# Two attentions: the first row maxima of the next step in front of this step's value products, and the low parts of queries and keys between a step's halves

## The chip, the core and the metric

The kernel is one program on one core of a Trainium2 chip. The metric is the time of one execution on the device, in microseconds (us), the median of several runs. Engine names are those of the profile: PE is TensorE (matmuls), PEld its weight loads, DVE is VectorE, ACT is ScalarE, POOL is GpSimd, SP is SyncE, which here issues DMAs only.

## What is computed

Two pre-norm transformer layers on an input of 16 batches x 512 positions x 128 values (float32). Layer 0 is causal attention (16 heads of 8) and a mixture of 8 experts of which each position takes two; layer 1 is attention without a mask and without an output projection, then a gated feed-forward network (FFN) on values rounded to 4-bit blocks. The change touches the two attentions alone:

```python
x = x + attn0(layernorm(x))    # layer 0
...
x = x + attn1(layernorm(x))    # layer 1
# attn0: q, k, v = split(x @ w_attn.T + b_attn)
#        w = softmax(where(tril, q @ k.T * 8**-0.5, -1e9));  (w @ v) @ w_proj.T + b_proj
# attn1: w = softmax((x @ w_Q) @ (x @ w_K).T / sqrt(8));      w @ (x @ w_V)
```

## The kernel before, in words

**Stages.** In time, the main loop of layer 0's attention fills about 100 to 850 us of the span, the experts 850 to 1215, layer 1's attention 1230 to 2010, the FFN the rest. Both attentions are built by the same function, `attention(layer)` (from line 558), with `causal` true for layer 0.

**Groups and steps.** The main loop (line 1256) goes over 64 groups: 16 batches, each with G = 4 groups of four heads. A group has NC = 4 steps `kc`, one for each chunk of 128 keys; the running number of a step is `now = NC * n + kc`. So a batch is 16 steps. A batch has two halves of two groups, each with its own tiles of queries and keys.

**Row maxima.** The softmax subtracts each row's exact maximum, which is found ahead: while the scores of group n are made, the maxima of group n + LEAD (LEAD = 3) are. `row_max` (from line 895) makes, for one chunk of 128 queries, matmuls `ps_max<-k,q` on 64 rows, two strips at a time, and DVE's `tensor_reduce` (L911) takes the maxima from PSUM to `mx`. In layer 0 two bf16 matmuls `ps_max<-mask_bf,ident_bf` add the mask to the last 128 columns. A chunk's maxima come in one or two *parts* (function `parts`), according to how many columns are left under the mask: one part holds both head pairs, if they fit into 512 columns together. In layer 1 there are always two. A step kc takes the chunk 3 - kc, so in layer 0 the maxima of steps 0 and 1 have two parts, of steps 2 and 3 one.

**From maxima to queries.** When a half's maxima are complete, `max_done` puts two things on the lists below: `part_max` (on DVE: `ml`, a copy and a difference that split the maxima into a high and a low part) and `put_max` (PE transposes `ps_mx`, an ACT copy and DMAs into spare rows of the query tile, so that the score matmul itself subtracts the maximum).

**Scores and values.** `score(kc, pairs)` makes two PSUM tiles `ps_sc` (64-row matmuls), then ACT's exponential `pt` (an `ACTIVATE`), and in layer 0 POOL's `affine_select` (L969), which zeroes what lies above the diagonal. `attend(kc)` is the value product: eight matmuls `ps_av<-pt,va` of 128 rows x 32 columns, in a tile `ps_av` that is held for a whole group; `leave` copies it to `av_sb` by ACT. `divide` (PE transposes to `ps_d`, DVE reciprocal and product) makes `at`. In layer 0 `turn_back` and `finish` make the output projection (`ps_t`, `ps_o`) and add it on DVE. In layer 1 `finish` is one POOL addition (L1041), followed two steps later by the LayerNorm and the quantization for the FFN (`quantize_after`; POOL's `ln_rstd` L204, `xn` L221, and `grid` L878).

**PSUM.** `for_dve` takes tiles of two banks from a ring of two (`ps_s`): all `ps_max`, `ps_d`, and in layer 0 also `ps_qk`, `ps_v`, `ps_o`, `ps_n`. `for_act` takes single banks from a ring of four (`ps_c`): `ps_sc`, `ps_av`, `ps_mx`, `ps_t`, in layer 1 also `ps_qk` and `ps_v`. A tile waits until the tile two (or four) places before it in its ring has been read.

**Who orders the work.** The helper `in_order` chains each instruction to the one before it on the same engine, so PE runs exactly in the order in which the Python code issues the matmuls, and POOL's larger operations likewise. In layer 0 DVE, ACT and POOL are chained wholly (`strict`); in layer 1 a scheduler places most of DVE's and ACT's instructions, while the reductions stay chained. Every matmul is recorded on line 294 (helper `mm`), every chained DVE or ACT operation on line 177, so that tiles, not lines, tell them apart.

**Lists of side work.** Everything that is not maxima, scores or value products hangs on three dictionaries by step: `soon` runs at the start of a step, `later` between the two halves of a step, `last_of` at its end. In layer 0 the prologue of batch b (LayerNorm `stats`, `moments`, `apply`; `both`, which makes `ps_qk` and the high parts `hi`; `low`, which makes the low parts `lo` on DVE from the same PSUM tile and sends them by DMA; and others) is entered at offsets from T = 16 (b - 2); `both` at T + 10 in `last_of`, `low` at T + 11 in `soon`.

**One step before the change**, in PE's order: `soon`; first part of the maxima of this step; first part of its scores; at kc = 2 the division of an earlier group (in layer 0 here, in layer 1 at the end of the step, by `last_of`); `later`; second parts of the maxima and scores; `last_of`; and then the value product of the step before (`behind`). The next step begins with its `soon` and its first maxima.

Of the kernel before, what the change touches and what calls it, by code (L numbers as in the profile page):

```python
# [36 lines left out]
def transformer_kernel(  # L37
# [25 lines left out]
    NC = S // P  # L63
# [79 lines left out]
    first = cp.tile([P, NE], F32, name="first")  # L143
# [165 lines left out]
    def table(name, shape, dtype=F32):  # L309
        return cp.tile(shape, dtype, name=name)  # L310

    steps = table("steps", [P, 1, NT], I32)
# [245 lines left out]
    def attention(layer):  # L558
        causal = layer == 0
# [28 lines left out]
        def for_dve(name):  # L588
            return ps_s.tile([P, 2, S], F32, tag="s", name=name)

        def for_act(name):
            return ring["act"](name)
# [294 lines left out]
        def strip(j):  # L887
            return slice(64 * j, 64 * (j + 1))
# [52 lines left out]
        def main_parts(b, g):  # L941


            hv = halves[b, g // 2]
            va = state[b]["va"]
            pts = {}
            acc = {}

            def score(kc, pairs):
                q0 = kc * P if causal else 0  # L950
                n = S - q0
                m = len(pairs)
                tiles = [for_act("ps_sc") for j in range(2)]
                for u, i in enumerate(pairs):
                    p = 2 * (g % 2) + i
                    for j, ps in enumerate(tiles):
                        r = strip(j)
                        mm(
                            ps[:, u * n : (u + 1) * n],
                            hv["k"][r, p, kc * P : (kc + 1) * P], hv["q"][r, p, q0:S],  # L960
                        )
                for j, ps in enumerate(tiles):
                    pt = pool.tile([P, S], F32, tag="pt", name="pt", bufs=12 if causal else 8)
                    act.activation(pt[:, 0 : m * n], ps[:, 0 : m * n], AF.Exp, scale=SCALE)
                    if causal:

                        head = pt[:, 0 : m * n].rearrange("p (u n) -> p u n", u=m)[:, :, 0:P]
                        in_order(
                            nc.gpsimd.affine_select(  # L969
                                head, head, pattern=[[0, m], [1, P]], base=0,  # L970
                                channel_multiplier=-1, compare_op=ALU.is_ge, fill=0.0,
                            ),
                            queue="pool",
                        )
                    for u, i in enumerate(pairs):
                        pts[kc, i, j] = pt[:, u * n : (u + 1) * n]

            def attend(kc):
                if kc == 0:
                    acc[0] = for_act("ps_av")  # L980
                av = acc[0]
                q0 = kc * P if causal else 0
                for i in range(2):
                    for j in range(2):
                        s = 2 * j + i
                        mm(
                            av[32 * s : 32 * (s + 1), q0:S],
                            va[:, kc, NP * j + 2 * g + i, :],
                            pts.pop((kc, i, j)),
                            start=kc == 0, stop=kc == NC - 1,  # L990
                        )

            def leave():
                t = pool.tile([P, S], F32, tag="av_sb", name="av_sb")
                act.copy(t, acc.pop(0))
                return t

            return score, attend, leave
# [25 lines left out]
        def finish(b):  # L1024
            at = state[b]["at"]
            xf = xs[b].rearrange("p c e -> p (c e)")
            if causal:
                aT = state[b]["aT"]
                ps = for_dve("ps_o")
                for c in range(NC):  # L1030
                    mm(ps[:, c // 2, EG * (c % 2) : EG * (c % 2 + 1)],
                       aT[:, c * P : (c + 1) * P], wo)
                p4 = ps[:, :, 0 : 2 * EG].rearrange("p b (c e) -> p b c e", e=EG)
                x4 = xs[b].rearrange("p (b c) e -> p b c e", b=2)
                vec.tensor_tensor(x4, x4, p4[:, :, :, 0:E], ALU.add)
                raw = state[b]["raw"]
                raws[b] = raw
                r4 = raw.rearrange("p (b c) e -> p b c e", b=2)
                vec.tensor_tensor(r4, r4, p4[:, :, :, E:EG], ALU.add)
            else:  # L1040
                in_order(nc.gpsimd.tensor_tensor(  # L1041
                    xf, xf, at.rearrange("p c e -> p (c e)"), ALU.add
                ), queue="pool")
            del state[b]


        LEAD = 3
# [7 lines left out]
        def max_steps(n):  # L1055
            if n >= len(groups):
                return []
            b, g = groups[n]
            return [
                [(lambda c=c, u=u: row_max(b, g, c, u)) for u in parts(c + 1)]  # L1060
                for c in reversed(range(NC))
            ]

        def max_done(n, step=None):
            if n < len(groups) and n % 2 == 1:
                at = groups[n][0], (n % G) // 2
                if step is None:
                    part_max(*at)
                    put_max(*at)
                else:  # L1070
                    soon.setdefault(step, []).append(lambda: part_max(*at))
                    later.setdefault(step + (not causal), []).append(lambda: put_max(*at))


        soon, later, last_of = {}, {}, {}
        pro = {}
        if causal:
# [43 lines left out]
            for b in range(2, B):  # L1121
                if b not in pro:
                    pro[b] = prologue(b)
                T = NC * G * (b - 2)
                for name, at, when in (
                    ("stats", -13, later), ("moments", -9, later), ("apply", 2, later),
                    ("biased", 3, later), ("turn", 6, later), ("values", 7, later),
                    ("both", 10, last_of), ("low", 11, soon), ("first", 13, later),
                    ("second", 16, later),
                ):  # L1130
                    if T + at >= 0:
                        when.setdefault(T + at, []).append(pro[b][name])
        else:
# [40 lines left out]
            rows = [f for n in range(LEAD) for fs in max_steps(n) for f in fs]  # L1174
# [72 lines left out]
        def quantize_after(b, step):  # L1247

            f = fp4_steps(b)
            for name, d in (  # L1250
# [2 lines left out]
            ):  # L1253
                later.setdefault(step + d, []).append(f[name])

        for n, (b, g) in enumerate(groups):
            nxt = n + LEAD
            steps = max_steps(nxt)
            score, attend, leave = main_parts(b, g)
            for kc in range(NC):  # L1260
                now = NC * n + kc
                maxima = steps.pop(0) if steps else []
                scores = [lambda u=u: score(kc, u) for u in parts(NC - kc)]
                for f in soon.pop(now, []):
                    f()
                if maxima:
                    maxima.pop(0)()
                scores.pop(0)()
                if kc == 2 and left:
                    bb, gg, t = left.pop(0)  # L1270
                    if not causal:
                        last_of.setdefault(now, []).append(lambda a=(bb, gg, t): divide(*a))
                    else:
                        divide(bb, gg, t)
                    if gg == G - 1 and causal:
                        later.setdefault(now + 1, []).append(lambda bb=bb: turn_back(bb))
                        at = now + 3
                        later.setdefault(at, []).append(lambda bb=bb: finish(bb))
                        gate_after(bb, at)
                    elif gg == G - 1:  # L1280
                        soon.setdefault(now + 1, []).append(lambda bb=bb: finish(bb))
                        quantize_after(bb, now + 1)
                for f in later.pop(now, []):
                    f()
                for f in maxima + scores:
                    f()
                for f in last_of.pop(now, []):
                    f()

                while behind:  # L1290
                    behind.pop(0)()
                behind.append(lambda kc=kc, f=attend: f(kc))
            behind.append(lambda b=b, g=g, f=leave: left.append((b, g, f())))
            max_done(nxt, NC * (n + 1))
        while behind:
            behind.pop(0)()
        for bb, gg, t in left:
# [499 lines left out]
```

## Time and profile before

| | before |
|---|---|
| median of 5 runs | 2254.33 us (2250.7 to 2255.74) |
| the profiled execution | 2254.83 us |
| its span in the profile | 2253.1 us |
| its granted TensorE clock | 0.964 |
| busy PE / PEld / DVE / ACT / POOL | 90 / 45 / 73 / 58 / 46% |
| the chain of work that ended last: PE / DVE / ACT / POOL | 36 / 13 / 4 / 2% |

The costliest groups of the attentions, with the page's columns: line, engine, operation, tiles, count, then busy us and mean ns of one, then idle time ahead of them and its commonest releaser:

```profile
L911 DVE TENSOR_REDUCE mx<-ps_max 128x2 f32<-128x1024 f32 (+1 forms) x896 | 1005.5, 1144 | 259.3 <-PE ps_max L294 256.7
L177 ACT ACTIVATE pt<-ps_sc 128x512 f32<-128x512 f32 (+2 forms) x1792 | 895.9, 570 | 442.4 <-PE ps_sc L294 413.0
L294 PE MATMUL ps_av<-pt,va 128*32 128x512 f32 (+3 forms) x4096 | 482.6, 530 | 11.7 <-POOL pt L969 8.1
```

A tile name on the left of the arrow is written, the names on the right are read; "128*32" is the shape of the weights on the array. The count is over the whole program, both layers. Matmuls are pipelined, so a duration on PE reaches into the next matmul; what a matmul costs the queue is read better from the interval between the starts of two that follow each other.

### The profile page before, as it was taken

How to read it: one execution, taken by the hardware profiler on the slowest of the kernel's cores; microseconds unless marked ns; L12 is line 12 of the kernel's file. 1: busy time of each engine (PE TensorE's matmuls, PEld its weight loads, DVE VectorE, ACT ScalarE, POOL GpSimd, SP SyncE). 2: the span in 40 equal slices, each digit the busy share in tenths (PEclk: the TensorE clock that was granted, in tenths of full speed). 3: DMA queues.
4: the chain of work that ended last, by engine and by line, in shares of the span. 5: the costliest groups of instructions: out<-in, count | busy, mean ns of one | idle time of the engine just before them, and what ended most of it. 6: DMA issues, size and time to landing. Idle time of an engine off the chain costs nothing.

```text
span 2253.1 us, 38218 instructions
## 1 busy us (share of the span) xinstructions
PE 2025.5 (90%) x13140; PEld 1019.3 (45%) x13140; DVE 1648.0 (73%) x2994; ACT 1299.0 (58%) x2564; POOL 1026.4 (46%) x1641
## 2 busy tenths in 40 slices
PE   6999999999999964989998999999999999995887
PEld 3444444444444432656665433333333333333665
DVE  6667676767767757946434888888888888845887
ACT  1566556656555642322334777777777777782443
POOL 3444746566574663132202355555455454115554
PEclk7999999999999976999999999999999999997999
DMA  7411222322222203555553222322222222100000
GB/s 191 113 60 60 77 78 88 94 75 73 66 76 83 58 25 99 148 154 143 157 152 98 69 69 78 92 82 72 85 69 68 69 69 70 57 2 3 22 24 28
DMA packets 148736, 180.15 MB, mean 80 GB/s; under 512 B 25647, under 2 KB 112784, under 8 KB 140352
## 3 DMA queue, kind: packets, MB, share of 16 engines
q1 hardware_dynamic: 139614, 160.26, 24.2%
q0 software_dynamic: 8352, 17.20, 2.7%
q8 instruction: 105, 1.72, 0.3%
q14 instruction: 87, 0.71, 0.1%
q10 hardware_dynamic: 578, 0.26, 0.1%
HBM read 116.55 MB, written 58.99 MB: 78 GB/s over the span
## 4 chain that ended last, share of the span: by engine, by line
PE 36%; DVE 13%; ACT 4%; POOL 2%; issue 1%; DMA 0%; SPq 0%; ACTq 0%; POOLq 0%
PE ps_av L294 10%; PE ps_sc L294 6%; PE ps_max L294 6%; DVE mx L911 5%; PE ps_y L294 4%; PE ps_h L294 4%; DVE hid L177 4%; ACT pt L177 3%; PE ps_d L297 2%; PE ps_qk L294 1%; POOL hid L177 1%; DVE f_mx L177 1%; PE ps_t L297 1%; DVE ml L177 1%; PE ps_v L294 1%
## 5 line engine op out<-in xcount | busy, mean ns | idle before, releaser
L911 DVE TENSOR_REDUCE mx<-ps_max 128x2 f32<-128x1024 f32 (+1 forms) x896 | 1005.5, 1144 | 259.3 <-PE ps_max L294 256.7
L177 ACT ACTIVATE pt<-ps_sc 128x512 f32<-128x512 f32 (+2 forms) x1792 | 895.9, 570 | 442.4 <-PE ps_sc L294 413.0
L294 PE MATMUL ps_sc<-q,k 64*128 64x512 f32 (+3 forms) x2048 | 479.3, 403 | 34.0 <-ACT pt L177 32.4
L294 PE MATMUL ps_av<-pt,va 128*32 128x512 f32 (+3 forms) x4096 | 482.6, 530 | 11.7 <-POOL pt L969 8.1
L294 PE MATMUL ps_max<-k,q 64*128 64x512 f32 (+3 forms) x2048 | 426.8, 433 | 26.2 <-DVE mx L911 19.1
L294 PEld LDWEIGHTS ps_max<-k,q 64*128 64x128 f32 x2048 | 185.8, 188 | 442.6 <-issue 175.4
L969 POOL TENSOR_SCALAR_AFFINE_SELECT pt<-pt 128x128 f32<-128x128 f32 (+1 forms) x768 | 247.2, 334 | 290.8 <-ACT pt L177 275.0
L294 PEld LDWEIGHTS ps_sc<-q,k 64*128 64x128 f32 x2048 | 230.1, 186 | 183.8 <-ACT pt L177 120.4
L1490 ACT ACTIVATE h<-ps_h,b1t 128x512 f32<-128x512 f32 x156 | 106.9, 687 | 192.7 <-PE ps_h L294 192.3
L1414 POOL DMA_INDIRECT got<-y_rows,backs x128 | 124.8, 975 | 99.5 <-DMA y_rows<-yt 63.6
L204 POOL TENSOR_TENSOR ln_rstd<-ln_ve,mhalf 128x4 f32<-128x4 f32 x62 | 63.9, 1030 | 202.6 <-DVE ln_nm L177 178.8
L294 PE MATMUL ps_y<-w2t,h 128*128 128x128 f32 x1248 | 148.6, 278 | 7.5 <-DVE yt L1504 7.5
L294 PE MATMUL ps_h<-xT,w1t 128*128 128x512 f32 x312 | 151.5, 618 | 2.5 <-DVE xT L305 1.3
L294 PEld LDWEIGHTS ps_y<-w2t,h 128*128 128x128 f32 x1248 | 144.4, 194 | 10.2 <-DVE yt L1504 8.0
L294 PEld LDWEIGHTS ps_av<-pt,va 128*32 128x32 f32 x4096 | 86.5, 108 | 137.3 <-issue 79.2
L533 POOL DMA_INDIRECT x_rows<-xg,slots x128 | 126.7, 990 | 25.5 <-issue 21.3
L294 PE MATMUL ps_max<-mask_bf,ident_bf 128*128 128x128 bf16 (+1 forms) x768 | 126.8, 248 | 0.0
L177 DVE SCALAR_TENSOR_TENSOR hid<-f_a,hid 128x704 f32<-128x704 f32 x64 | 78.6, 1229 | 22.5 <-ACT f_a L177 22.5
L297 PE MATMUL ps_d<-cst,av_sb 128*128 128x128 f32 x512 | 84.5, 288 | 6.7 <-DVE mx L911 5.2
L294 PEld LDWEIGHTS ps_h<-xT,w1t 128*128 128x128 f32 x312 | 51.1, 192 | 77.1 <-ACT h L1490 53.3
L294 PE MATMUL ps_gu<-wgT,xqT 128*128 128x352 f32 x128 | 53.7, 502 | 33.0 <-DVE hid L177 33.0
L177 ACT COPY av_sb<-ps_av 128x512 f32<-128x512 f32 x128 | 76.2, 595 | 11.4 <-PE ps_av L294 2.5
(242 smaller groups left out, 2140.9 us busy)
## 6 DMA issues: line engine op xcount, KB each, us to landing
q<-d SPq DMA_DIRECT2D x256, 128.0 KB
k<-d SPq DMA_DIRECT2D x256, 128.0 KB
d<-hi SPq DMA_DIRECT2D x64, 256.0 KB
d<-lo SPq DMA_DIRECT2D x64, 256.0 KB
xt<-x_rows SPq DMA_DIRECT2D x39, 262.0 KB
w1t<-in_w_dram SPq DMA_DIRECT2D x39, 256.0 KB
w2t<-in_w_dram SPq DMA_DIRECT2D x39, 256.0 KB
y_rows<-yt SPq DMA_DIRECT2D x39, 256.0 KB
```

What stands on the lines that cost most here:

```text
L177: ins = f(*args, **kw)
L204: in_order(nc.gpsimd.tensor_tensor(rstd, ve, mhalf, ALU.pow), queue="pool")
L294: return in_order(nc.tensor.matmul(out, lhsT, rhs, start=start, stop=stop))
L297: return in_order(nc.tensor.transpose(out, src, ident))
L533: ins = in_order(nc.gpsimd.indirect_dma_start(out=x_rows[:, :], out_offset=bass.IndirectOffsetOnAxis(ap=slots[:, b0 + u, k, c : c + 1], axis=0
L911: nc.vector.tensor_reduce(hv["mx"][:, c, :, p0 : p0 + m], s4, AX.X, ALU.max),
L969: nc.gpsimd.affine_select(head, head, pattern=[[0, m], [1, P]], base=0, channel_multiplier=-1, compare_op=ALU.is_ge, fill=0.0,),
L1414: ins = in_order(nc.gpsimd.indirect_dma_start(out=got[:, c, :], out_offset=None, in_=y_rows[0 : min(NT, NE * (b + 1)) * TS, :], in_offset= ...
L1490: nc.scalar.activation(h[:, f, :], ps, AF.Gelu, bias=t["b1"][:, f : f + 1])
```

## The change

The loop gets a helper `first_maxima(now)`, which runs `soon` of the step `now` and issues the first part of its maxima. It is called once ahead of the loop, and then, for the step now + 1, at the end of step now: after its scores and `last_of`, in front of the value product of the step before. In layer 1 the steps that end with a division (kc = 2, by `last_of`) keep the old order: there it is called after the value product (`turned`). `max_done` is called at the start of a group and not at its end. In layer 0 `low` goes from `soon` to `later`, so behind the first part of that step's maxima and of its scores. In layer 1 `finish` goes from `soon` to `later` of the same step.

```diff
-                    ("both", 10, last_of), ("low", 11, soon), ("first", 13, later),
+                    ("both", 10, last_of), ("low", 11, later), ("first", 13, later),
...
+        maxima = []
+        def first_maxima(now):
+            for f in soon.pop(now, []):
+                f()
+            n, kc = divmod(now, NC)
+            if kc == 0:
+                rows[:] = max_steps(n + LEAD)
+            if rows:
+                maxima[:] = rows.pop(0)
+                maxima.pop(0)()
+        rows = []
+        first_maxima(0)
         for n, (b, g) in enumerate(groups):
             nxt = n + LEAD
-            steps = max_steps(nxt)
             score, attend, leave = main_parts(b, g)
+            max_done(nxt, NC * (n + 1))
             for kc in range(NC):
                 now = NC * n + kc
-                maxima = steps.pop(0) if steps else []
                 scores = [lambda u=u: score(kc, u) for u in parts(NC - kc)]
-                for f in soon.pop(now, []):
-                    f()
-                if maxima:
-                    maxima.pop(0)()
                 scores.pop(0)()
...
-                        soon.setdefault(now + 1, []).append(lambda bb=bb: finish(bb))
+                        later.setdefault(now + 1, []).append(lambda bb=bb: finish(bb))
                         quantize_after(bb, now + 1)
                 for f in later.pop(now, []):
                     f()
                 for f in maxima + scores:
                     f()
+                maxima.clear()
+                turned = now in last_of and not causal
                 for f in last_of.pop(now, []):
                     f()
+                if not turned:
+                    first_maxima(now + 1)
                 while behind:
                     behind.pop(0)()
+                if turned:
+                    first_maxima(now + 1)
                 behind.append(lambda kc=kc, f=attend: f(kc))
             behind.append(lambda b=b, g=g, f=leave: left.append((b, g, f())))
-            max_done(nxt, NC * (n + 1))
```

## The prediction

> **What bounds the kernel now.** I read the busy table by stretches first, then the waits, then the timeline of single steps. Stretch 100 to 850 us is the causal attention of layer 0, 1230 to 2010 us the attention of layer 1; columns are stretch, length, then busy PE, PEld, DVE, ACT, POOL, clock, DMA share, GB/s.
>
> ```profile
> 100.00:850.00 750.00, 696.17 (x5365) 335.57 (x5357) 515.85 (x1166) 439.98 (x970) 432.67 (x995) 0.97 0.23 72
> 1230.00:2010.00 780.00, 734.04 (x4535) 292.94 (x4531) 672.57 (x1010) 603.71 (x1154) 358.65 (x404) 1.00 0.23 70
> ```
>
> TensorE is busy 93 and 94%, so its own order sets the end; in layer 1 VectorE (86%) and ScalarE (77%) have little to spare, in layer 0 they have much (69 and 59%). The reader is to see that a matmul saved counts at once in layer 0, and that in layer 1 every wait put in front of TensorE counts too. The waits view (waiter, releaser: sum us, mean ns, longest us) shows on whom TensorE waits: ScalarE's exponentials for `ps_sc`, VectorE's reduction for `ps_max`.
>
> ```profile
> PEld ps_max L294 <- DVE mx L911: 117.1, 173, 1.8
> PE ps_sc L294 <- ACT pt L177: 32.4, 121, 4.5
> ```
>
> The timeline (start, duration) of one causal seam between two steps, and of the maxima behind it:
>
> ```profile
> 446.43 0.87 PE L294 MATMUL ps_sc<-q,k 64*128 64x512 f32 x2
> 447.23 0.43 PE L294 MATMUL ps_av<-pt,va 128*32 128x128 f32 x8
> 447.58 0.45 PE L294 MATMUL ps_max<-k,q 64*128 64x384 f32 x2
> 447.96 0.28 PE L294 MATMUL ps_max<-mask_bf,ident_bf 128*128 128x128 bf16 x2
> 448.18 0.44 PE L294 MATMUL ps_sc<-q,k 64*128 64x384 f32 x2
> ```
>
> **What moves.** Set against each other engine by engine, the two programs have the same instructions. ScalarE, the DMA queues, the MoE and the FFN keep their order. TensorE has only the first maxima of a step and the value product in front of them swapped: in layer 0 at 153 seams directly and at 88 with another operation between them; in layer 1 at 182 seams of 242, the 60 with a division staying. VectorE has the low parts behind the first reduction at 14 places; GpSimd has the residual add of layer 1 (L1041) behind `ln_rstd`/`grid` instead of ahead, 15 times. So I price seams.
>
> **Layer 0, a plain seam.** Undisturbed intervals from start to start: before, `ps_sc` to `ps_av` .424, to `ps_max` .355, to the mask .371, to `ps_sc` .215, sum 1.365. After: `ps_sc` to `ps_max` .335 (as inside a step), to the mask .265, mask to `ps_av` .215 (not shown; taken as mask to `ps_sc`), `ps_av` to `ps_sc` .355 (as to `ps_max`): 1.170. The .195 are two changes of tile shape fewer, each about .1: three 64-row products in a row instead of two pairs. The other two seam kinds come out likewise, 2.119 to 1.919 and 1.578 to 1.373. Bounds of a seam: 0, if the mask pays the change that the maxima save, to .30, if mask to `ps_av` costs nothing of it. Of 153 seams, 14 are low steps and 17 wait for GpSimd; 122 x .195 = **-23.8 us** (0 to -37). The 88 others exchange like for like: nothing.
>
> **Layer 0, waits that go.** At 17 seams the product before 128x512 waits for `affine_select`:
>
> ```profile
> 461.33 1.40 PE L294 MATMUL ps_av<-pt,va 128*32 128x512 f32 x8
> 462.66 0.50 PE L294 MATMUL ps_max<-k,q 64*128 64x256 f32 x4
> ```
>
> With the maxima ahead (.433 + .322 with mask) the wait holds that work: 10 long ones x .755 + 7 short ones (.34 to .44) x .36 = **-10.1**. Five or six maxima that follow the product now wait .58 on VectorE's `ml`; in front they are fed earlier: **-3**. No wait is late next there: the slot that they need came free in the step before.
>
> **Layer 0, waits that come.** Low parts: today the product stands between the scores and the maxima that need VectorE's low parts.
>
> ```profile
> 285.41 1.41 DVE L177 SCALAR_TENSOR_TENSOR lo<-ps_qk,bp,hi 128x512 fp32r<-128x512 f32 x2 [2.88 <-ACT hi L177]
> 285.85 0.64 PE L294 MATMUL ps_av<-pt,va 128*32 128x256 f32 x8
> 286.88 0.50 PE L294 MATMUL ps_max<-k,q 64*128 64x512 f32 x2 [0.39 <-DVE lo L177]
> ```
>
> The changed order has the next maxima, and with them the `ps_s` slot that a low part holds, ahead of the product; queued behind them are the product and the next scores. The .57 that the product covered (285.85 to the maxima's unstalled start) comes back, 14 x .57 = **+8.0** (0 to +18: the upper end adds the reduction of 128x512, mean .69, that VectorE now does ahead of the low parts). The `ps_n` seams wait for the division's slot, 7 x .2 = **+1.4**; seams whose maxima wait for a VectorE slot already (14 x .25 = **+3.5**) and seams that gain just ahead of a GpSimd- or VectorE-limited place (10 x .2 = **+2**) lose their cover. Layer 0: -23.8 - 10.1 - 3 + 8.0 + 1.4 + 3.5 + 2 = **-22 us** (-34 to -8).
>
> **Layer 1, a plain seam.** Without a mask both orders have one 64-row block a step, so no shape change is saved (1.92 both ways). The step is paced by VectorE (2 reductions x 1.22 of a 3.19 us step), ScalarE (2 x .57 and copies) and two PSUM slots. Where the second scores wait for an exponential, maxima inside that wait gain .06. What moves is cover:
>
> ```profile
> 1538.32 1.26 POOL L878 TENSOR_TENSOR grid<-q_a,xn 128x512 bf16<-128x512 f32 x1
> 1538.44 1.19 DVE L177 CAST ml<-mx 128x32 fp32r<-128x32 f32 x1
> ...
> 1539.62 1.06 PE L294 MATMUL ps_av<-pt,va 128*32 128x512 f32 x8
> 1539.66 0.21 DVE L177 TENSOR_TENSOR ml<-mx,ml 128x32 fp32r<-128x32 f32 x1
> 1539.80 2.34 DVE L911 TENSOR_REDUCE mx<-ps_max 128x2 f32<-128x1024 f32 x2
> ...
> 1541.07 0.50 PE L294 MATMUL ps_max<-k,q 64*128 64x512 f32 x2 [0.38 <-DVE mx L911]
> 1541.40 0.39 PE L294 MATMUL ps_sc<-q,k 64*128 64x512 f32 x2
> ```
>
> The maxima at 1541.07 wait until the reduction begun at 1539.80 has freed their slot (about 1541.0). Today the product at 1539.62 runs inside that wait. Swapped, it stands behind it: maxima 1541.07, product 1541.43, scores 1542.43 instead of 1541.40, so 1.03 us lost; queued behind are the scores, both exponentials and `av_sb`. I replayed one batch (1535 to 1586 us) by hand, each tile at the latest of its engine, its slot and its input. In it this place loses 1.03, three others .19, .33 and .09 (an `ml`, a `q_a` and small slot waits), and later waits of .70 and .47 take .45 back: 1.19 a batch; the 14 batches between the first and the last x 1.19 = **+16.7** (0, if all is taken back as the .45 was, to +25, if nothing is).
>
> The residual add now comes to GpSimd directly behind `grid`, at 1539.58; VectorE's second `ml` operation comes at 1539.66. Where the two met in layer 0, VectorE took 1.22 for what takes .21 here:
>
> ```profile
> 408.22 1.27 POOL L800 TENSOR_TENSOR x<-x,b_bc 128x512 f32<-128x512 f32 x1
> 408.32 1.22 DVE L177 TENSOR_TENSOR ml<-mx,ml 128x32 fp32r<-128x32 f32 x1
> ```
>
> At the same boundary today (`grid`, then `xn`), 5 of 13 such `ml` operations were slowed. The add comes .08 ahead, so I take a little more, .45, at the full price: 13 x .45 x 1.08 = **+6.3** (0 to 14). The Trainium skill ("SBUF — State Buffer", section "SBUF: two separate sides") speaks against the change here: VectorE with two SBUF inputs and GpSimd share a port pair as an exclusive lock, and whichever starts first blocks the other for the whole instruction. By that rule the add, .08 ahead, would hold `ml` in every batch, and the sum would be 14 and not 6.3. Layer 1: 16.7 + 6.3 = **+23 us** (+5 to +33).
>
> **Sum.** -22 + 23 = +1 on the profiled execution's 2254.83 us (span 2253.1), .5 above the median 2254.33: **2256 us**, the gain of layer 0 paid back in layer 1. Own range 2247 to 2264.
>
> **Rivals.**
> - Regained (faster): in layer 1 the waits of the next steps absorb the late product. For it: the .45 regained in the replay, and 117.1 us of weight loads waiting on `mx`, so the reduction stream, not the product, paces some steps. Against: that stream is itself behind the late maxima. Layer 1 costs +6, layer 0 gives -22: 2239 (2236 to 2247).
> - Blocked and thin (slower): the add blocks `ml` in all 13 batches, +14, and layer 0 saves only 12, because the GpSimd chain behind its products (17 wait for it today) and VectorE's slots give gains back. One mechanism decides the sign: `ml` behind the add, just ahead of the reductions that feed layer 1's maxima; it decides once over 9 of 13 are blocked. 2254.8 - 12 + 30.7 = 2273.5 (2264 to 2277). For it: 408.22. Against: 8 of 13 went through beside `xn`.
> - The shape change isn't saved (the change doesn't do what it says): mask to `ps_av` takes .41, not .215, as the first product after 64-row scores does. Then -23.8 falls away: 2256 + 23.8 = 2280. Against: mask to `ps_sc` at .215 follows the same tile.
>
> **Numbers.** About .2%, 4.5 us, is what a measurement tells from no change. Forecast .42 (of it .09 faster, .20 same, .13 slower); regained .29, faster; blocked and thin .23, slower; not saved .06, slower. Faster .38, same .20, slower .42. The range 2236 to 2277 leaves out "not saved" and the tails of the bounds, about 2 in 10.
>
> **What would show it.** In layer 0 mask to `ps_av` near .2 and two batches in about 96.5 us (99.2 now); maxima of low steps waiting for `lo` with the product behind them. In layer 1 a batch period of 52.5 us, against 50.86 now, and the product behind the maxima in the place of 1539.62; `ml` at 1.2 in half of the batches. Wrong if layer 1's period stays, or if mask to `ps_av` is .4; and if ScalarE's waits for `ps_sc` grow in layer 0, a bound that I left out is at work.

## The result and the profile after

The changed kernel takes **2260.4 us** (median; 2254.0 to 2269.5) against 2254.65 before: ratio 1.0031, 95% interval 1.0023 to 1.0039. It is slower by .3%, just clear of what a measurement tells from no change. The forecast was 2256, its own range 2247 to 2264. The single number hides what happened; the two loops show it. Columns are stretch (first to last value product of a layer), length, busy PE, PEld, DVE, ACT, POOL, clock, DMA share, GB/s. Before:

```profile
64.88:821.96 757.08, 725.46 (x5599) 348.05 (x5597) 524.80 (x1141) 458.33 (x1009) 426.56 (x1016) 0.99 0.23 72
1225.37:2025.38 800.01, 752.00 (x4634) 298.92 (x4635) 677.13 (x1019) 619.07 (x1184) 362.86 (x407) 1.00 0.23 70
```

After:

```profile
65.28:781.97 716.69, 694.59 (x5592) 343.31 (x5591) 520.73 (x1140) 454.96 (x1008) 423.72 (x1014) 0.99 0.25 76
1185.93:2030.66 844.73, 782.94 (x4631) 307.91 (x4633) 687.83 (x1019) 612.09 (x1183) 361.06 (x407) 0.98 0.22 66
```

Layer 0 is **40.4 us shorter** (forecast -22) and layer 1 **44.7 us longer** (forecast +23). Both signs were right, and both sizes were forecast at about half of what came; both measurements lie outside the bounds that the prediction gave them (-34 to -8, +5 to +33). That the time came near 2256 is luck: the two errors, 18 us too little gain and 22 us too little loss, cancel.

The profiled execution took 2258.97 us, its span is 2257.3. Its waits follow, in the columns of the prediction's waits view (waiter, releaser: sum us, number of waits, longest us; the prediction takes the middle column for a mean, but it is a count). The first line is of the kernel before, the others of the changed one:

```profile
PE ps_max L294 <- DVE mx L911: 19.1, 44, 0.9
...
PE ps_sc L294 <- ACT pt L177: 39.4, 151, 4.5
PEld ps_max L294 <- DVE mx L911: 79.9, 130, 2.5
PE ps_max L294 <- DVE mx L911: 37.3, 39, 2.2
```

TensorE's own waits for VectorE's reduction went from 19.1 to 37.3 us, fewer and longer (39 of them, .96 each). In layer 1 alone they went from 13.3 to 28.0, so this wait grew by 14.7 us where the layer lost 44.7. The weight loads' share fell, so the sum over the program would have said little. The place is found by step. With a step counted as `now` mod 16 within a batch, and its length from the first scores of one step to those of the next, means over ten batches in the middle of each loop (us):

| kernel | layer 1: step 4 | 5 | 6 | the other 13 | ml's second operation |
|---|---|---|---|---|---|
| before | 3.36 | 2.90 | 3.98 | 40.7 | .21 to .40 |
| after | 5.68 | 3.81 | 3.53 | 41.3 | 1.20 to 1.21 |

and in layer 0, where a batch went from 49.50 to 46.82: step 4 -.43, 8 and 9 together -.67, 10 -.47, 11 -.60, 12 -.19, 15 -.15, all others within .11.

**Layer 0's seam**, in the timeline of TensorE (start, duration), after the change:

```profile
417.73 0.56 PE L294 MATMUL ps_sc<-q,k 64*128 64x512 f32 x2
418.07 0.40 PE L294 MATMUL ps_max<-k,q 64*128 64x384 f32 x2
418.40 0.28 PE L294 MATMUL ps_max<-mask_bf,ident_bf 128*128 128x128 bf16 x2
418.62 0.42 PE L294 MATMUL ps_av<-pt,va 128*32 128x128 f32 x8
418.97 0.45 PE L294 MATMUL ps_sc<-q,k 64*128 64x384 f32 x2
```

The product starts .22 after the mask, as forecast, and not .41: the shape change is saved. The second of the two score matmuls starts .07 after the first; from it to the next scores the seam takes 1.18. The prediction had 1.365 for it before the change and 1.170 after.

**Layer 1's place**, the step 4 of a batch:

```profile
1570.91 1.27 POOL L878 TENSOR_TENSOR grid<-q_a,xn 128x512 bf16<-128x512 f32 x1
1571.03 1.19 DVE L177 CAST ml<-mx 128x32 fp32r<-128x32 f32 x1
...
1572.15 1.26 POOL L1041 TENSOR_TENSOR x<-x,at 128x512 f32<-128x512 f32 x1
1572.26 1.20 DVE L177 TENSOR_TENSOR ml<-mx,ml 128x32 fp32r<-128x32 f32 x1
1573.39 3.47 DVE L911 TENSOR_REDUCE mx<-ps_max 128x2 f32<-128x1024 f32 x3
...
1574.66 0.50 PE L294 MATMUL ps_max<-k,q 64*128 64x512 f32 x2 [2.19 <-DVE mx L911]
...
1575.09 1.06 PE L294 MATMUL ps_av<-pt,va 128*32 128x512 f32 x8
```

Read it downward: both GpSimd operations hold one operation of `ml` each until they end (1572.18, 1573.41); the first reduction starts 2.4 us after `ml` began; the maxima wait 2.19 for it; and the product, which waits for nothing here, stands behind them with nothing of its 1.06 in the wait.

**The clock behind the wait.** Step 5 is longer for another reason. Here are steps 4 and 5 of this batch, and below them those of the batch two later, in the columns of the stretches above (the clock is the third number from the end, as a share of full speed):

```profile
1570.79:1576.09 5.30, 2.92 (x21) 1.01 (x18) 5.23 (x6) 2.06 (x4) 4.35 (x7) 1.00 0.00 0
1576.09:1580.41 4.32, 4.32 (x24) 1.57 (x21) 3.49 (x7) 3.17 (x6) 0.00 (x0) 0.60 0.02 6
1679.75:1685.04 5.29, 2.91 (x21) 1.01 (x17) 5.22 (x6) 2.06 (x4) 4.35 (x7) 1.00 0.00 0
1685.04:1687.96 2.92, 2.92 (x24) 1.21 (x21) 2.92 (x7) 2.78 (x6) 0.00 (x0) 1.00 0.00 0
```

In both, TensorE is busy through the whole of step 5 with the same work. At a granted clock of 0.60 it takes 4.32, at 1.00 it takes 2.92, which is the 2.90 of before. In the trace the clock stands at 0.50 for 3.41 us (1576.27 to 1579.68). Such a fall comes in 12 of the 16 batches of layer 1, each time after the wait for `ml`; in layer 1 of the kernel before there is none. The mid-loop batches with a fall take 54.4 to 54.6 us, the one without 53.03: 1.4 us a fall, so some 17 of the 44.7 us. The falls begin at whole multiples of 3.413 us from each other (1521.65, 1576.27 and 1630.88 are 16 x 3.413 apart), whatever the batch does, which may be why a wait of the same length is followed by a fall in one batch and not in another. No run sets the clock by itself: that the wait brings the fall is read from their order and from the counts below, and is not tested apart.

### The profile page after: what moved, and what is told of

The parts are those of the page before. It is cut to its first block, busy times and chain, and to the rows that moved or that the text cites. A ratio compares the mean times of both kernels' runs of the same rounds, so it can differ in the third digit from the quotient of the medians.

```text
span 2257.3 us, 38218 instructions
## 1 busy us (share of the span) xinstructions
PE 2025.6 (90%) x13140; PEld 1024.0 (45%) x13140; DVE 1655.7 (73%) x2994; ACT 1289.9 (57%) x2564; POOL 1022.6 (45%) x1641
## 4 chain that ended last, share of the span: by engine, by line
PE 41%; DVE 11%; ACT 4%; POOL 2%; issue 1%; DMA 0%; ACTq 0%; POOLq 0%; DVEq 0%
PE ps_av L294 11%; PE ps_sc L294 9%; PE ps_max L294 6%; PE ps_h L294 4%; PE ps_y L294 4%; DVE hid L177 4%; ACT pt L177 3%; DVE mx L911 2%; PE ps_d L297 2%; PE ps_qk L294 1%; DVE ml L177 1%; POOL hid L177 1%; DVE f_mx L177 1%; PE ps_t L297 1%; PE ps_mx L297 1%; PE ps_v L294 1%
## 5 line engine op out<-in xcount | busy, mean ns | idle before, releaser
L911 DVE TENSOR_REDUCE mx<-ps_max 128x2 f32<-128x1024 f32 (+1 forms) x896 | 995.3, 1143 | 214.9 <-PE ps_max L294 210.4
L294 PE MATMUL ps_sc<-q,k 64*128 64x512 f32 (+3 forms) x2048 | 520.4, 428 | 40.9 <-ACT pt L177 39.4
L294 PE MATMUL ps_max<-k,q 64*128 64x512 f32 (+3 forms) x2048 | 436.4, 414 | 42.7 <-DVE mx L911 37.3
L294 PEld LDWEIGHTS ps_sc<-q,k 64*128 64x128 f32 x2048 | 236.8, 187 | 451.2 <-ACT pt L177 311.7
L294 PEld LDWEIGHTS ps_max<-k,q 64*128 64x128 f32 x2048 | 203.1, 190 | 204.1 <-DVE mx L911 79.9
L177 DVE RECIPROCAL rec<-ps_d 128x16 f32<-128x16 f32 x128 | 32.6, 255 | 105.3 <-PE ps_d L297 105.2
```

Source lines behind the costliest of these rows:

```text
L177: ins = f(*args, **kw)
L294: return in_order(nc.tensor.matmul(out, lhsT, rhs, start=start, stop=stop))
L911: nc.vector.tensor_reduce(hv["mx"][:, c, :, p0 : p0 + m], s4, AX.X, ALU.max),
```

## The experiments

Two theories for layer 1. **Lock**: the residual add behind `grid` holds `ml`, and that is the loss. **Cover**: whatever `ml` takes, the maxima in front of the product wait with nothing beside them. For layer 0 the question was where 18 us more than forecast came from. All runs are against the kernel before on the same chip, its medians 2253.9 to 2254.2, but for the last two.

**One layer at a time.** Layer 0 alone, layer 1 in its old order:

```diff
-                turned = now in last_of and not causal
+                turned = not causal
...
-                        later.setdefault(now + 1, []).append(lambda bb=bb: finish(bb))
+                        soon.setdefault(now + 1, []).append(lambda bb=bb: finish(bb))
```

> Layer 0 as in the change, layer 1 in its old order (first maxima behind the value product, residual add ahead of grid). If the two layers act by themselves, as the stages of the two traces say (layer 0 shorter by 40, layer 1 longer by 45): 2254.7 - 40 = 2214 us. If a part of layer 0's gain is only work put off into the experts or layer 1: above 2222 us.

Measured 2217.7 us, ratio .9836 (.9812 to .9860). Layer 1 alone (`turned = causal or now in last_of`, `low` in `soon`):

> Layer 1 as in the change, layer 0 in its old order with the low parts in soon. If the layers act by themselves: 2254.7 + 45 = 2300 us, ml's second operation 1.2 us in nearly every batch. If layer 1's loss comes from what layer 0 leaves behind (its earlier end, the experts' reads): nearer to 2255 us.

Measured 2296.2 us, ratio 1.0185 (1.0171 to 1.0199). -36.6 and +41.9 make +5.3, close to the change's own 5.8: the layers act by themselves, and nothing is put off from one into the other.

**The add alone, and the swap without it.** The change with `finish` in `soon`:

> The whole change, but layer 1's residual add stays ahead of grid on GpSimd. Theory lock alone (the add behind grid holds ml's second operation, and this is all of layer 1's loss): 2260.4 - 45 = 2215 us. Theory cover alone (the first maxima wait for the reduction in front of the product, whatever ml takes): 2260 us. Both: ml's second operation back at 0.2 us, the reductions 1.0 earlier in 14 batches, so 2260.4 - 14 = 2246 us, with step 4 of a batch at 4.7 us (3.36 before, 5.68 after).

Measured 2241.4 us, ratio .9943 (.9928 to .9958). The kernel before with `finish` in `later` and nothing else:

> The kernel before with nothing but layer 1's residual add put behind grid. Theory lock alone: ml's second operation 1.2 us in nearly every batch and the whole loss of layer 1, 2300 us. Both: the product in front of the maxima covers what it can, but reductions that are 1.0 late can't be covered further, 2254.7 + 14 = 2269 us. Theory cover alone: 2255 us.

Measured 2267.2 us, ratio 1.0061 (1.0046 to 1.0075). Each theory alone is out; both act. The clock falls in seven batches of the first kernel and in one of the second. In this kernel the product stands in front of the maxima, and of the wait that `ml` makes it takes its 1.06:

```profile
1592.96 1.06 PE L294 MATMUL ps_av<-pt,va 128*32 128x512 f32 x8
1593.00 1.24 DVE L177 TENSOR_TENSOR ml<-mx,ml 128x32 fp32r<-128x32 f32 x1
...
1595.43 0.50 PE L294 MATMUL ps_max<-k,q 64*128 64x512 f32 x2 [1.40 <-DVE mx L911]
```

**The old order at one seam.** In layer 1 the product first wherever the maxima follow a split:

```diff
-                turned = now in last_of and not causal
+                turned = not causal and (now in last_of or now % 8 == 3)
```

> The whole change, but in layer 1 the two steps of a batch that follow a split of maxima (steps 4 and 12) keep the product in front of the maxima, as the steps with a division do. Theory lock and cover at step 4: step 4 falls from 5.68 to 4.3 and step 5 from 3.8 to 3.0, step 6 rises from 3.5 to 3.9, so 1.8 a batch: 2260.4 - 25 = 2235 us. Theory that every swapped step of layer 1 pays (cover lost all over): some 2 of 12 swapped steps, 2260.4 - 7 = 2253 us.

Measured 2259.2 us, ratio 1.0024 (1.0013 to 1.0036), step 4 still 5.68. A miss: this turns the seam that leads into step 4, and the wait falls at the seam out of it, as the prediction's own lines had it. With `now % 16 == 4` in its place:

> The whole change, but in layer 1 the one seam of a batch at which the wait falls (from step 4 to step 5) keeps the product in front of the maxima; in ml_turned the old order stood one step too early, and nothing moved. Theory cover at this seam: steps 4, 5 and 6 as in finish_alone (4.31, 3.03, 3.92; now 5.68, 3.81, 3.53), 1.76 a batch: 2260.4 - 25 = 2236 us. Theory that the lock alone makes step 4 late: 2258 us or more.

Measured 2240.9 us, ratio .9927 (.9907 to .9947): step 4 4.24, as expected, step 5 3.60 and not 3.03, step 6 3.53 and not 3.92. The clock falls in four batches (step 5 takes 4.06 to 4.21 there). In the others step 5 takes 3.35, and steps 4 to 6 together 11.11, against 11.17 in the kernel with the add alone and 11.74 in the changed one: the old order at this seam gives back what the swap had cost there, and step 5 only holds what step 6 held. One seam of a batch carries some 20 of the 45 us. By the batches with and without a fall, some 13 of these 20 are the clock (4 falls of .9 us in place of 12 of 1.4).

**No lock at all.** Layer 0 alone as above, and `grid` behind the four `xn` on GpSimd:

```diff
-                ("inverse", 10), ("scaled", 12), ("size", 14), ("least", 15), ("down", 15), ("grid", 16),
+                ("inverse", 10), ("scaled", 12), ("size", 14), ("least", 15), ("down", 15), ("grid", 18),
```

> The change in layer 0 alone, and layer 1 in its old order but with grid behind the four xn on GpSimd. If what is left of the lock (ml's copy, 1.19 beside grid) holds up step 4, it goes: step 4 from 3.38 to 2.9, 2217.7 - 7 = 2211 us. If the copy is hidden anyway: 2217 us.

Measured **2204.6 us**, ratio .9775 (.9762 to .9788), better than both kernels. `ml` takes .20 and .25, step 4 2.84, as step 12 does; step 6 falls to 3.54 too, which had not been expected. So the lock was in the kernel before already, for 11 us (its layer 1 goes from 800.0 to 788.8). The whole change with the same two GpSimd orders:

> The whole change in both layers, but on GpSimd the residual add stays ahead of grid, and grid comes behind the four xn, so that neither operation of ml meets a long GpSimd one. Theory that the cover is needed only because ml is held: the swap is nearly free in layer 1, step 4 near 2.9, and the small terms of the other steps (.6 a batch, 8 us) stay: 2204.6 + 9 = 2214 us. Theory that the cover is lost whatever ml takes: step 4 at 4.3 or more and 2204.6 + 28 = 2233 us.

Measured 2216.7 us, ratio .9834 (.9822 to .9847). With `ml` free the swap costs .50 at step 4 (3.34 against 2.84), and the clock doesn't fall:

```profile
1549.60 0.20 DVE L177 CAST ml<-mx 128x32 fp32r<-128x32 f32 x1
1549.84 0.25 DVE L177 TENSOR_TENSOR ml<-mx,ml 128x32 fp32r<-128x32 f32 x1
...
1551.27 0.49 PE L294 MATMUL ps_max<-k,q 64*128 64x512 f32 x2 [0.24 <-DVE mx L911]
```

Together the runs make a table of layer 1, first to last value product, with the number of falls of the clock in brackets. The last column is an estimate: it takes off each fall at what the batches with it took more than those without it in the same run (1.42 us in the swapped order, .9 in the old one).

| `ml` held by | old order | swapped | the swap costs | without the falls |
|---|---|---|---|---|
| nothing | 788.8 (0) | 803.6 (0) | 14.9 | 14.9 |
| `grid` | 800.0 (0) | 827.2 (7) | 27.2 | 17.3 |
| `grid` and the add | 813.8 (1) | 844.7 (12) | 31.0 | 14.8 |

Down a column the lock costs 25 in the old order and 41 in the swapped one; without the falls it is 24 in both, and the price of the swap hardly changes with the lock. That it seems to double is the clock. The falls go with the length of the wait ahead of step 4's last maxima: none where it is .6 us or less, four falls in 12 waits of 1.2 us (the old order at step 4's seam), one in 12 of 1.4 us (the add alone), seven in 12 of 1.4 us (the change with the add ahead of `grid`), and in the changed kernel eleven in 12 of 2.2 us and one more behind a wait of 1.4 us. Why equal waits of 1.4 us bring one fall in one run and seven in the other is open. Of the 14.9, .50 a batch are at step 4, and most of the rest at .07 to .18 in steps 2, 3, 10, 11, 14 and 15.

**The low parts.** The kernel before with `low` in `later`:

> The kernel before with nothing but the low parts put into later (the order of the maxima and products stays). Theory slot of the low parts (the prediction's: the next first maxima take the PSUM slot that the low parts read, wherever these stand): the low parts come .69 later behind a reduction and the maxima with them, 2254.5 + 14 x .7 = 2264 us. Theory slot by release (the maxima take the slot that is given back first in program order, which is now that of the 128-wide maxima): the .46 wait goes, 2254.5 - 6 = 2248 us, step 11 at 1.59 us as step 15 has it (2.04 before).

Measured 2254.4 us, ratio .9995 (.9986 to 1.0004): neither. The wait goes as the theory by release says (step 11 1.59), but step 12 gives it back (3.54, before 3.10): `ml` now stands behind the low parts on VectorE, and the transposes `ps_mx` wait for it. The change with `low` in `soon`:

> The whole change, but the low parts stay in soon, so ahead of the reduction of the 128-wide maxima. Theory slot by release: the next first maxima, now in front of the product, need the slot of the low parts, and wait for the second of them; step 11 goes from 1.44 to about 1.8 us or more, 2260.4 + 5 = 2265 us or more. Theory slot of the low parts (that wait is in the changed kernel already): not slower than 2260 us, rather 2251.

Measured 2279.7 us, ratio 1.0115 (1.0100 to 1.0131); step 11 2.61, far more than the 1.8 expected. Its lines:

```profile
419.98 1.41 DVE L177 SCALAR_TENSOR_TENSOR lo<-ps_qk,bp,hi 128x512 fp32r<-128x512 f32 x2 [1.65 <-ACT hi L177]
...
421.44 0.50 PE L294 MATMUL ps_max<-k,q 64*128 64x512 f32 x2 [0.95 <-DVE lo L177]
...
422.08 0.64 PE L294 MATMUL ps_av<-pt,va 128*32 128x256 f32 x8
```

And the changed kernel's:

```profile
413.94 0.69 DVE L911 TENSOR_REDUCE mx<-ps_max 128x4 f32<-128x512 f32 x1 [1.04 <-PE ps_max L294]
...
414.55 1.41 DVE L177 SCALAR_TENSOR_TENSOR lo<-ps_qk,bp,hi 128x512 fp32r<-128x512 f32 x2
...
414.89 0.45 PE L294 MATMUL ps_max<-k,q 64*128 64x512 f32 x2
```

Here the maxima start at 414.89, while the low parts read `ps_qk` until 415.96. They can't be in that slot: they have the one that the reduction gave back at 414.63. With the low parts ahead of the reduction in the code, the maxima get `ps_qk`'s slot and wait, with the product behind them. So the move of the low parts is worth nothing to the old order and 19 us to the new one.

**The projection behind step 10.** The change with the product first at layer 0's seam from step 9 to 10 (`turned = now in last_of and not causal or causal and now % 16 == 9`):

> The whole change, but in layer 0 the seam from step 9 to step 10 of a batch, after which queries and keys are projected, keeps the product in front of the maxima. Theory slot of ps_qk (its PSUM slot is given back by the reduction of these maxima, so maxima that come a product earlier free it earlier): ps_qk waits again, .95 us after ps_d instead of .49, and the seam's change of shape comes back, steps 9 to 10 up by .46 + .15 in 14 batches, 2260.4 + 8.5 = 2269 us. Theory that the projection's wait has another cause (ScalarE, the division): + .15 x 14 = 2262.5 us, with ps_qk at .49 after ps_d.

Measured 2374.3 us against 2347.5 of the kernel before on this chip, ratio 1.0118 (1.0098 to 1.0137). Once more:

> The kernel of qk_turned once more, since on the chip of that run the kernel before took 2347.5 us itself and layer 1 had a halt of some 7 us a batch that no other run shows. If layer 0's steps there (9 and 10 up by 1.22 a batch, ps_qk at .95) stand for themselves: 2260.4 + 14 x 1.22 = 2277 us here. If that chip's halt was also in them: 2269 us, as expected at first.

Measured 2363.0 against 2344.0 on another such chip, ratio 1.0078 (1.0057 to 1.0099), .5% over the change's 1.0031. On these two chips layer 1 loses 6 to 7 us a batch at steps 13 to 15 in this kernel; layer 0's steps agree with the changed kernel's to .03 but for 5 (+.07) and the two in question, so those are read, and the total is not settled by these runs. Step 9 goes from 4.33 to 4.94 (the seam's shape change and the wait for GpSimd that the maxima had covered), step 10 from 4.31 to 4.93 (without a fall of the clock from 4.21 or 4.28 to 4.78), and the projection waits again:

```profile
417.79 0.66 PE L297 MATMUL ps_d<-cst,av_sb 128*128 128x128 f32 x4
418.74 0.70 PE L294 MATMUL ps_qk<-xnT,wp 128*128 128x512 f32 x1 [0.29 <-DVE mx L911]
```

.95 after `ps_d`, against .49 in the changed kernel: it waits for the slot that the reduction of step 10's maxima gives back.

## Why the prediction was right, and where it was not

- **The exchange as a whole: right**, layer 0 faster, layer 1 slower, the sum near nothing. The one-layer runs show it.
- **Layer 0, plain seams: right.** Mask to product .215 and product to scores .355 are as assumed. From the second score matmul to the next scores, the seam that the prediction works out (steps 0, 4 and 12) has a median of 1.37 before and 1.175 after, so .195 as forecast; at step 15 the change saves .15. The rival "not saved" is out.
- **Layer 0, low parts: the sign was wrong** (+8.0; measured -.46 a batch, some -6). The step that failed is "the `ps_s` slot that a low part holds": the prediction took the two slots to go round in turn, as the section on PSUM ahead of it does. They go by which is given back first in the order of the code, and that is what the move of `low` changes. The price it feared is real, in the kernel that leaves `low` in `soon`.
- **Layer 0, a term left out:** `ps_qk` comes .46 earlier behind `ps_d`, since its slot is freed by maxima that now come a product earlier; with what hangs on it step 10 saves .47, x 14 = 6.6 us. The prediction had priced the 88 seams with another operation between as like for like.
- Take both off, and layer 0's rest is -40.4 + 6.4 + 6.6 = -27.4 against the -30 of the other terms (waits that go and come among them). The clock falls here too, for 17.1 us before and 13.7 after, so it decides little.
- **Layer 1, cover: right in mechanism and in size.** 1.19 a batch was forecast, 16.7 in all. With `ml`'s copy held, as in the kernel before, the swapped batches without a fall of the clock take 52.25, against 50.94: 1.31 more, some 18 in all. Step 4 lost 1.13 (1.03 forecast), and the .45 came back at step 6.
- **Layer 1, a term left out: the clock.** The prediction read a clock of 1.00 for this loop and kept it. Twelve falls at 1.42 us are 17 us, most of the 22 us by which layer 1's loss went beyond the forecast.
- **Layer 1, the add: right in kind, the wrong row chosen.** 6.3 forecast; `ml` was held in 12 of 13 batches, and the add cost 13.8 in the old order and 17.5 in the swapped one (12.9 and 10.4 without the falls, by the table). The 5 of 13 beside `xn` were the wrong row: `xn` is four operations of .44, and the most that it held `ml` is .40, where the add is one of 1.26. The rule of the Trainium skill ("SBUF — State Buffer", section "SBUF: two separate sides"), which the prediction weighed and set aside, is the better account: the add came .11 ahead and held `ml` to its end, here and in the run with the add alone.
- **Rivals.** Blocked and thin: its first half came (12 batches of 13; layer 1 lost even more), its second turned round, since layer 0 saved more and not less. Regained: only at steps 6 and 7 (.55 a batch).

## What to carry to other kernels

An engine whose order is fixed hides a wait by what stands in front of it: before a ready product is put behind an operation that may wait, look for the places where that wait is longest today, and price two things there. One is the cover that goes: here .5 to .7 us a batch over steps 4 to 6, with a wait of .24, 1.4 or 2.2 us alike. The other is the granted clock behind the longer wait: here 1.4 us each time it falls, so read the clock column step by step and not as a mean. And price the two parts of a swap by stage: a change that is worth nothing as a whole may be worth 1.6% in one loop and cost about as much in the other, and can be taken where it pays. A slot ring that hands out whatever is given back first makes the order of the *readers* part of every edit.

## What the runs showed of the hardware

A small VectorE operation next to a GpSimd `TENSOR_TENSOR` of 1.27 us took 1.19 to 1.24 instead of .20, and ended with it; next to GpSimd's .44 us operations it took at most .40. The kernel before pays 11 us for it. No wait names this; it shows only where the duration of an operation is set beside the same operation's elsewhere.

TensorE's granted clock fell to 0.50 for 3.41 us behind single waits of 1.2 to 2.2 us, while the mean clock of layer 1 went only from 1.00 to 0.98. In the changed kernel a step that was all TensorE work took 4.32 with the fall and 2.92 without.

On two of the chips the kernel before took 2344 and 2347.5 us, 4% more. In one batch of layer 1 there, ScalarE stood still for about 5 us in step 13, with no releaser shown, while GpSimd issued indirect DMAs; why is open.
